# Turning rows and contexts round: 64 TensorE transposes replaced by VectorE squares of 32 and small transfers, in a four-layer cross-attention kernel

## The chip, the core and the metric

The kernel runs on one core of a Trainium2 chip. The metric is device time in microseconds (us); smaller is better. The engines are TensorE (PE in the profile, with PEld for its weight loads), VectorE (DVE), ScalarE (ACT), GpSimd (POOL) and SyncE (SP, which here only issues DMA transfers). The kernel before took 1388.54 us, the median of three runs (1388.54 to 1392.53).

## The reference

Four layers, each an attention of 4 x 256 tokens (256 wide) over a context of 4 x 512 vectors (128 wide), then a feed-forward part. All is float32. Cut to what matters here:

```python
x = x + L0_xattn(layernorm(x), ctx, ...)   # 16 heads of 16, normalised heads, context split in two parts
x = x + L0_ffn(layernorm(x), ...)          # 64 arrows, the best 4 of each token
x = x + L1_xattn(layernorm(x), ctx, ...)   # 16 heads of 128 over 8 groups of keys and values
x = x + L1_ffn(layernorm(x), ...)          # 8 experts, 2 for each token, and a shared one
x = x + L2_xattn(layernorm(x), ctx, ...)
x = x + L2_ffn(layernorm(x), ...)          # one of two experts for each token
x = x + L3_xattn(layernorm(x), ctx, ...)
x = x + L3_ffn(layernorm(x), ...)          # 64 chosen tokens of each batch
```

A layer norm takes each token's row of 256, subtracts its mean and divides by its standard deviation. Every product with such rows on TensorE needs them turned round, with the 256 numbers along the partitions; the attention's products with the context need that turned round as well.

## The kernel before, in words

**Rows and how they are turned.** x stays in SBUF, a tile `x_sb[b]` of [128 partitions, 2, 256] for each of four batches. `Norm(b, name)` (line 908 on) takes mean and variance on VectorE and the reciprocal root on GpSimd (line 922); its `tokens()` writes the normalised rows, a tile of tag "xn" (line 927). `layernorm_T` (line 933) turns such a tile round: four TensorE transposes of 128x128 into one PSUM bank (line 939), then a copy by ScalarE into a tile of tag "xnT" (line 942). Both tags lie in the pool `lnp`, which has two buffers for each tag. `context_T` (line 901) turns a batch's context in the same way (lines 905 and 906) into `cT`.

**Order.** TensorE, ScalarE, VectorE and GpSimd run their instructions in the order in which the program writes them (a manual schedule). SyncE's transfers are placed by the scheduler. Transfers go round eight DMA semaphores, 100 to 107 in the trace, and a transfer that takes a semaphore waits for the one that used it last. A tile that takes over a buffer waits for every instruction and transfer that used the tile before it there.

**Layer 0's attention.** For each batch b there are eight slots i (four head groups, two halves of the keys each). A slot puts scores on TensorE (line 1373), calls `ahead(b, i)`, puts the products with the values of the head group before (lines 1383 and 1392), in odd slots `quotient` on VectorE (lines 1406 to 1414), and then calls `between(b, i)`, which holds steps of the next batch n = b + 1: in slot 0 the rows and the context of n are turned and `last_context` copies a part of the context on GpSimd (line 1172); in slot 1 `project_q` (line 1184) multiplies the turned rows by the query weights; in slot 2 `project_k`, in slot 3 `project_v` and sums; `scaled` (line 1271) and `transposed` follow, whose evacuations are lines 1348 to 1364. In slots 5 to 7 the norm and the rows of batch n + 1 are made. PSUM is a ring of six banks beside two for the products with the values; scores take four banks of the ring at a time.

**Attentions 1 to 3.** 32 units (batch b, pair of heads hp from 0 to 7). In a unit the queries of the next unit are made (`seven`, line 1882; `four`, lines 1891 to 1895), then the scores (line 1912), the exponentials on ScalarE (line 1915), the products with the context (line 1920). At hp 1 the next batch's norm is taken, at hp 3 its rows are made, at hp 5 they are turned, at hp 6 `x_sums` (lines 1813 to 1816) makes sums of their blocks on VectorE, and the queries of (b + 1, 0) read them during unit (b, 7). At hp 3 and 7 the output of four pairs is made as well.

**Layer 1's experts** (`beside1`): beside batch b of attention 1, batch b - 1's norm is taken at hp 3, its rows at hp 4; at hp 5 `turned1` stores the rows in DRAM (line 2179) and turns them (lines 2184 and 2185); at hp 6 `chosen` picks the experts. Beside batch 0, weights are loaded by SyncE, two transfers for each unit (`load_waiting`).

Of the kernel before, what the change touches and what calls it, by code (L numbers as in the profile page):

```python
# [9 lines left out]
F32 = mybir.dt.float32  # L10
# [7 lines left out]
P = 128  # L18
B, S, D = 4, 256, 256
# [817 lines left out]
def bounded_path(ctx: ExitStack, tc: tile.TileContext, t, out: bass.AP, over):  # L837
# [63 lines left out]
    def context_T(b):  # L901

        pt = bank("t", [P, NK, P], f"pcT{b}")
        for k in range(NK):
            nc.tensor.transpose(pt[:, k, :], c_sb[:, b, k, :], ident)
        nc.scalar.copy(cT[:, b, :], pt.rearrange("p k q -> p (k q)"))
# [38 lines left out]
    def layernorm(b, name, keep=None):  # L945
        xn = Norm(b, name).tokens(keep)
        return xn, layernorm_T(xn, name)

    def normalised(name):

        after = layernorm(0, f"{name}_0")
        for b in range(B):
            _, xnT = after
            if b + 1 < B:
                after = layernorm(b + 1, f"{name}_{b + 1}")
            yield b, xnT

    raws = {}

# [68 lines left out]
    with tc.manual_schedule(engines={E.PE, E.Activation, E.DVE, E.Pool}):  # L1028
# [552 lines left out]
        def between(b, i):  # L1581

            n = b + 1
            if n == 1:
                if i == 0:
                    for k0 in range(0, NK, 2):
                        project_k(n, k0)()
                    scale[n] = Scale(n)
                    scale[n].square(False, NC, NQK)
                    xnTs[n] = layernorm_T(xns[n], f"a0_{n}")  # L1590
                elif i == 1:
                    project_q(n)()
                    scale[n].square(False, 0, NC)
                    project_v(n)
                elif i == 2:
                    scale[n].sum()
                    scale[n].power()
                elif i == 5:
                    transposed(n, 0)
                    transposed(n, 2)  # L1600
                elif i == 6:
                    transposed(n, 4)
            elif n < B:
                if i == 0:
                    xnTs[n] = layernorm_T(xns[n], f"a0_{n}")
                    context_T(n)
                    last_context(n)
                elif i == 1:
                    project_q(n)()
                elif i == 2:  # L1610
                    for k0 in range(0, NK, 2):
                        project_k(n, k0)()
                    scale[n] = Scale(n)
                    scale[n].square(False)
                elif i == 3:
                    project_v(n)
                    scale[n].sum()
                elif i == 4:
                    scale[n].power()
                elif i == 6:  # L1620
                    transposed(n, 0)
                    transposed(n, 2)
            if n + 1 < B:
                if i == (5 if n == 1 else 6):
                    norms[n + 1] = Norm(n + 1, f"a0_{n + 1}")
                elif i == (6 if n == 1 else 7):
                    xns[n + 1] = norms[n + 1].tokens()

            i0 = 4 if b == B - 1 else 6
            if b > 0 and i in (i0, i0 + 1):  # L1630
                output0(b - 1, (i - i0,))
            if b == 1:
                if i == 0:
                    bias_rows()
                elif i == 1:
                    bias_columns()
                elif i == 2:
                    output_bias()
            if b == B - 1:
                if i == 0:  # L1640

                    mf = w0.tile([B * NK, P], F32, tag="hs", name="mf", bufs=1)
                    nc.vector.tensor_copy(mf, m8)
                    xns["mf"] = mf
                elif i == 1:
                    pmk = bank("mm", [P, B * NK], "pmk")
                    nc.tensor.transpose(pmk, xns["mf"], ident[: B * NK, : B * NK])
                    nc.vector.tensor_scalar(
                        mbias.rearrange("p b k -> p (b k)"), pmk, 1.0, -NEG, ALU.subtract, ALU.mult
                    )  # L1650
                elif i == 2:
                    score_bound()
                elif i == 3:

                    nc.vector.tensor_reduce(
                        quad[:, :32], ident.rearrange("p (a q) -> p q a", q=32), AX.X, ALU.add
                    )
                    for j in range(1, 4):
                        nc.vector.tensor_copy(quad[:, 32 * j : 32 * (j + 1)], quad[:, :32])
            if b == B - 1:  # L1660
                if i in (0, 2, 6):
                    norms["f", i // 2] = Norm(min(i // 2, 2), f"f0_{min(i // 2, 2)}")
                if i in (1, 3, 7):
                    xns["f", i // 2] = norms["f", i // 2].tokens()
                if i in (3, 5):
                    k = (i - 3) // 2
                    xnTs["f", k] = layernorm_T(xns["f", k], f"f0_{k}")
                if i == 4:
                    arrows[0] = Arrows(0)
                    arrows[0].vectors()  # L1670
                if i == 5:
                    arrows[0].routes()
# [111 lines left out]
    def attention(L, m_sb, n_sb, first_xnT=None, after=None, at_end=None, chunk=None, within=None):  # L1784
# [11 lines left out]


        with tc.tile_pool(name=f"att{L}", bufs=2) as ap:
            xnTs, xns, xxs, norms, qTs, pqs, outs, sums = {}, {}, {}, {}, {}, {}, {}, {}
            units = [(b, hp) for b in range(B) for hp in range(H // 2)]  # L1800
            m_x = ap.tile([P, H // 2, 3, P], F32, tag="m_x", name=f"m_x{L}", bufs=1)
            n_x = ap.tile([P, H // 2, 3, P], F32, tag="n_x", name=f"n_x{L}", bufs=1)
# [220 lines left out]
            for n, (b, hp) in enumerate(units):  # L2023
                if b + 1 < B:
                    if hp == 1:
                        norms[b + 1] = Norm(b + 1, f"a{L}_{b + 1}")
                    elif hp == 3:
                        xns[b + 1] = norms[b + 1].tokens()
                if n == 0:
                    first_queries(1)  # L2030
                    x_sums(0)
                elif n + 1 < len(units):
                    queries(*units[n + 1])
                if b + 1 < B and hp == 5:
                    xnTs[b + 1] = layernorm_T(xns[b + 1], f"a{L}_{b + 1}")
                if b + 1 < B and hp == 6:
                    x_sums(b + 1)
                if b == 0:
                    m_sums((hp + 2) % (H // 2))
                if n:  # L2040
                    summed(*units[n - 1], *half)

                last, i = ((b, 0), hp - 4) if hp >= 4 else ((b - 1, 1), hp)
                prev = last[0] >= 0
                h0 = 4 * last[1]
                if prev and i >= 2:
                    for k in (2 * i - 4, 2 * i - 3):
                        o_sums(last[0], h0 + k, nc.gpsimd)
                half = heads(b, hp)
                if prev and i == 0:  # L2050
                    quotients(*last)
                if prev and i in (1, 2):
                    for k in (2 * i - 2, 2 * i - 1):
                        divided(last[0], h0 + k, nc.gpsimd)
                if b == 0 and hp < 6:
                    n_sums(hp)
                if (b, hp) == (1, 0):
                    n_sums(6)
                    n_sums(7)
                if prev and i == 3:  # L2060
                    out = Output(*last)
                    if last != (B - 1, 0):
                        out.products()
                        out.add()
                if after:
                    after(b, hp)
# [108 lines left out]
    nc.vector.memset(taken[:, 0, :], 0.0)  # L2175
    xnT1 = {}

    def turned1(b, xn):
        nc.sync.dma_start(xd[b * S : (b + 1) * S, :].rearrange("(c p) d -> p c d", p=P), xn)
        xnT1[b] = fx.tile([P, ND, S], F32, tag=f"xnT{b}", name=f"xnT_f1_{b}")  # L2180
        pt = bank("t", [P, ND, S], f"pxn_f1_{b}")
        for c in range(NC):
            for d in range(ND):
                nc.tensor.transpose(pt[:, d, c * P : (c + 1) * P], xn[:, c, d * P : (d + 1) * P], ident)
        nc.scalar.copy(xnT1[b], pt)
# [51 lines left out]
    def beside1(b, hp):  # L2237
        if b == 0:
            load_waiting(2)
        if b > 0:  # L2240
            if hp == 3:
                ahead1[b] = Norm(b - 1, f"f1_{b - 1}")
            elif hp == 4:
                ahead1[b] = ahead1[b].tokens()
            elif hp == 5:
                turned1(b - 1, ahead1[b])
            elif hp == 6:
                chosen(b - 1)

# [1192 lines left out]
```

## Time and profile before

| what | value |
| --- | --- |
| median of 3 runs | 1388.54 us |
| the profiled execution's own time | 1389.42 us |
| its span in the profile | 1387.6 us |
| TensorE busy | 1374.4 us, 7261 matmuls |
| VectorE, GpSimd, ScalarE busy | 886.8, 684.8, 580.8 us |
| granted TensorE clock, mean | 0.998 |
| DMA packets | 50849, 47.10 MB |
| transposes of rows (line 939), all of attention's tiles | 64, 273 ns each in the group's row |
| SyncE's transfers | 153 |

A timeline line gives the start, the length, the engine, the line of the kernel, the operation, the tile it writes and those it reads, and how many instructions are merged; in brackets stands the idle time before it and what ended it. Matmuls are pipelined, so the durations of neighbours overlap. A "windows" line gives a stretch, its length, the busy time of each engine, then the granted TensorE clock and the share and rate of the DMA engines.

### The profile page before, as it was taken

The page shows a single profiled execution, that of the slowest core. Times are in us where ns is not written, and L with a number is a line of the kernel's source. Part 1 is how long each engine was busy: PE and PEld are TensorE (multiplying, and loading weights), DVE is VectorE, ACT ScalarE, POOL GpSimd, SP SyncE. Part 2 cuts the span into 40 slices and gives each one's busy share as a digit, 9 for nine tenths or more (in the row PEclk, how much of TensorE's full clock was granted, in tenths as well). Part 3 has the DMA queues.
Part 4 walks back from the last instruction along what each step waited for, and adds up shares of the span by engine and source line. Part 5 has one row for each costly group of instructions (what it writes and reads, how often), then busy time and mean ns, then how long its engine had stood idle before and what let it go on. Part 6 is the DMA issues. An engine that isn't in the chain of part 4 may idle for free.

```text
span 1387.6 us, 19978 instructions
## 1 busy us (share of the span) xinstructions
PE 1374.4 (99%) x7261; PEld 906.5 (65%) x7261; DVE 886.8 (64%) x2026; ACT 580.8 (42%) x1148; POOL 684.8 (49%) x829
## 2 busy tenths in 40 slices
PE   8999999999999999999999999999999999999998
PEld 7665676566656667887565666666875656666667
DVE  6667863666666557655666756558656758566675
ACT  5776454433343333256434333333264334333331
POOL 4223433466564445232577654556315675445561
PEclk9999999999999999999999999999999999999999
DMA  5000220300000000272110000000342000000001
GB/s 169 2 1 2 76 77 16 75 26 1 9 0 9 0 9 30 51 231 74 39 54 8 16 1 8 1 0 16 112 125 65 9 4 4 0 1 0 1 0 34
DMA packets 50849, 47.10 MB, mean 34 GB/s; under 512 B 8755, under 2 KB 46868, under 8 KB 50742
## 3 DMA queue, kind: packets, MB, share of 16 engines
q1 hardware_dynamic: 46838, 37.74, 9.2%
q0 software_dynamic: 2544, 6.95, 1.8%
q8 instruction: 60, 0.98, 0.3%
q10 hardware_dynamic: 1360, 1.05, 0.2%
q14 instruction: 47, 0.39, 0.1%
HBM read 38.78 MB, written 6.95 MB: 33 GB/s over the span
## 4 chain that ended last, share of the span: by engine, by line
PE 94%; POOL 2%; DVE 2%; DMA 1%; issue 1%; ACT 0%; DVEq 0%; ACTq 0%; POOLq 0%
PE ps L1912 23%; PE po L1920 23%; PE paq L1882 6%; PE pao L1882 5%; PE pbq L1882 4%; PE pbo L1882 4%; PE ps L1373 3%; PE po L1383 2%; PE paf L1457 2%; PE pyf L1507 2%; PE pgu L2459 2%; PE psh L2281 1%; PE py L2006 1%; PE pm L987 1%; PE pn L1003 1%
## 5 line engine op out<-in xcount | busy, mean ns | idle before, releaser
L1931 POOL TENSOR_TENSOR half<-pT 128x1024 f32<-128x1024 f32 x93 | 218.4, 2348 | 288.3 <-ACT pT L1915 215.9
L1912 PE MATMUL ps<-qT,cT 128*128 128x512 f32 x768 | 345.6, 593 | 0.0
L1920 PE MATMUL po<-pT,c_sb 128*128 128x512 f32 x768 | 345.3, 592 | 0.0
L1915 ACT ACTIVATE pT<-ps,mbias 128x512 f32<-128x512 f32 x384 | 264.0, 687 | 155.1 <-PE ps L1912 141.0
L1920 PEld LDWEIGHTS po<-pT,c_sb 128*128 128x128 f32 x768 | 145.8, 190 | 183.2 <-issue 183.2
L1912 PEld LDWEIGHTS ps<-qT,cT 128*128 128x128 f32 x768 | 138.9, 190 | 138.4 <-issue 136.3
L1924 ACT COPY oT<-po 128x512 f32<-128x512 f32 x96 | 56.3, 586 | 265.2 <-PE po L1920 265.2
L1967 POOL TENSOR_TENSOR oT<-oT,wide 128x512 f32<-128x512 f32 x84 | 106.8, 1292 | 0.0
L1892 DVE TENSOR_TENSOR qT<-qT,paq 128x128 f32<-128x128 f32 x90 | 25.5, 283 | 96.0 <-ACT qT L1891 96.0
L1377 ACT ACTIVATE pT<-ps 128x512 f32<-128x512 f32 x128 | 66.0, 602 | 26.3 <-PE ps L1373 26.0
L1939 DVE TENSOR_TENSOR half<-half 128x512 f32<-128x512 f32 x96 | 71.8, 748 | 2.7 <-POOL half L1929 2.5
L1941 DVE STREAM_TRANSPOSE turned<-half 128x512 f32<-128x512 f32 x96 | 68.3, 711 | 6.3
L1892 DVE TENSOR_TENSOR w<-w,pao 128x128 f32<-128x128 f32 x21 | 6.0, 285 | 103.0 <-ACT w L1891 103.0
L1882 PE MATMUL paq<-xnT_a,m_sb 128*128 128x128 f32 x360 | 71.4, 280 | 0.0
L1882 PE MATMUL paq<-xx,m_x 128*128 128x128 f32 x360 | 69.6, 275 | 0.0
L1882 PEld LDWEIGHTS paq<-xnT_a,m_sb 128*128 128x128 f32 x360 | 57.2, 192 | 16.7 <-issue 8.7
L1945 DVE TENSOR_REDUCE sums<-turned 128x16 f32<-128x512 f32 x96 | 65.9, 686 | 3.3
L1882 PE MATMUL pao<-n_x,ox 128*128 128x128 f32 x336 | 65.0, 275 | 0.0
L1891 ACT COPY qT<-paq 128x128 f32<-128x128 f32 x90 | 24.0, 266 | 94.0 <-PE paq L1882 93.0
L1895 DVE TENSOR_TENSOR qT<-qT,pbq 128x384 f32<-128x384 f32 x90 | 49.9, 554 | 9.7 <-DVE qT L1894 0.5
L1882 PEld LDWEIGHTS paq<-xx,m_x 128*128 128x128 f32 x360 | 54.7, 192 | 0.0
L1966 DVE STREAM_TRANSPOSE wide<-rz 128x512 f32<-128x512 f32 x84 | 54.4, 685 | 0.0
(490 smaller groups left out, 2545.7 us busy)
## 6 DMA issues: line engine op xcount, KB each, us to landing
wq<-in_L_wqT SPq DMA_DIRECT2D x11, 512.0 KB
wo<-in_L_wo SPq DMA_DIRECT2D x11, 512.0 KB
yd<-yr SPq DMA_DIRECT2D x20, 128.0 KB
xd<-xn_f SPq DMA_DIRECT2D x8, 256.0 KB
w<-in_F_w SPq DMA_DIRECT2D x4, 512.0 KB
wk<-in_L_wkT SPq DMA_DIRECT2D x11, 128.0 KB
wv<-in_L_wvT SPq DMA_DIRECT2D x11, 128.0 KB
yd<-yb SPq DMA_DIRECT2D x9, 128.0 KB
```

Source lines behind the costliest of these rows:

```text
L1377: nc.scalar.activation(pT[kp][:, j], ps[j], AF.Exp)
L1882: nc.tensor.matmul(p[:, at, :], lhsT=lhsT, rhs=rhs, start=(k == 0 and at == 0), stop=(k == len(of) - 1 and i == which[-1]),)
L1912: nc.tensor.matmul(ps, lhsT=cT[:, b, k * P : (k + 1) * P], rhs=qT, start=True, stop=True)
L1915: nc.scalar.activation(pT[:, k, :], ps, AF.Exp, bias=mbias[:, b, k : k + 1])
L1920: nc.tensor.matmul(po, lhsT=c_sb[:, b, k, :], rhs=pT[:, k], start=(k == 0), stop=(k == NK - 1))
L1924: done["head"] = nc.scalar.copy(raw, po).ins
L1931: nc.gpsimd.tensor_tensor(half, pT[:, 0:2], pT[:, 2:4], ALU.add)
L1939: nc.vector.tensor_tensor(part, half[:, 0], half[:, 1], ALU.add)
L1941: nc.vector.transpose(turned.rearrange("p f i -> p (f i)"), part)
L1945: nc.vector.tensor_reduce(sums[b, hp // 4][:, hp % 4, :], turned, AX.X, ALU.add)
L1966: nc.vector.transpose(wide, rzs[b, hp // 4][:, hp % 4, :, None].to_broadcast([P, NB, 32]))
L1967: eng.tensor_tensor(outs[b, hp], outs[b, hp], wide.rearrange("p f i -> p (f i)"), ALU.mult)
```

## The change

VectorE can turn squares of 32x32 within 32 partitions. The change turns rows in that way: one VectorE instruction for each half of a row tile turns all its squares and writes them, ordered by their destination, into a new tile of tag "xn"; then 16 transfers on SyncE's queue, each from 32 partitions to 32 partitions, bring the squares to the partitions where they belong. It is done for the rows of batches 1 to 3 in attentions 1 to 3, for batches 0 to 2 of layer 1's experts, and in layer 0 for the rows and the contexts of batches 2 and 3. The first batches keep their transposes.

The steps move with it. In layer 0 the next but one batch's context is turned in slot 3, its norm taken in slot 4, and its rows made and turned in slot 5 of the batch before; slot 0 keeps `last_context` only. In the attentions the rows are turned at hp 3, where they are made, and for the experts at hp 4.

```diff
-    def normalised(name):
...
+    def turned_aside(dst, src, name):
+
+        y = lnp.tile([P, 4, 4, 32], F32, tag="xn", name=f"y_{name}")
+        nc.vector.transpose(
+            y.rearrange("p q n s -> p n q s"), src.rearrange("p (n q s) -> p n q s", q=4, s=32)
+        )
+        to = dst.rearrange("p (n i s) -> p i n s", i=4, s=32)
+        for i in range(4):
+            for q in range(4):
+                nc.sync.dma_start(to[32 * q : 32 * q + 32, i], y[32 * i : 32 * i + 32, q])
+
+    def layernorm_aside(xn, name, dst=None):
+
+        xnT = lnp.tile([P, ND, S], F32, tag="xnT", name=f"xnT_{name}") if dst is None else dst
+        y = lnp.tile([P, 4, ND, NC, 32], F32, tag="xn", name=f"y_{name}")
+        for c in range(NC):
+            nc.vector.transpose(
+                y[:, :, :, c].rearrange("p q d s -> p d q s"), xn[:, c, :].rearrange("p (d q s) -> p d q s", d=ND, s=32)
+            )
+        to = xnT.rearrange("p d (c i s) -> p i d c s", c=NC, s=32)
+        for i in range(4):
+            for q in range(4):
+                nc.sync.dma_start(to[32 * q : 32 * q + 32, i], y[32 * i : 32 * i + 32, q])
+        return xnT
...
             elif n < B:
                 if i == 0:
-                    xnTs[n] = layernorm_T(xns[n], f"a0_{n}")
-                    context_T(n)
                     last_context(n)
...
             if n + 1 < B:
-                if i == (5 if n == 1 else 6):
+                if i == 3:
+                    turned_aside(cT[:, n + 1, :], c_sb[:, n + 1].rearrange("p k c -> p (k c)"), f"c{n + 1}")
+                if i == 4:
                     norms[n + 1] = Norm(n + 1, f"a0_{n + 1}")
-                elif i == (6 if n == 1 else 7):
-                    xns[n + 1] = norms[n + 1].tokens()
+                elif i == 5:
+                    xnTs[n + 1] = layernorm_aside(norms[n + 1].tokens(), f"a0_{n + 1}")
...
                     elif hp == 3:
-                        xns[b + 1] = norms[b + 1].tokens()
+                        xnTs[b + 1] = layernorm_aside(norms[b + 1].tokens(), f"a{L}_{b + 1}")
...
-                if b + 1 < B and hp == 5:
-                    xnTs[b + 1] = layernorm_T(xns[b + 1], f"a{L}_{b + 1}")
...
-    def turned1(b, xn):
+    def turned1(b, xn, aside=False):
...
+        if aside:
+            layernorm_aside(xn, f"f1_{b}", xnT1[b])
+            return
...
             elif hp == 4:
-                ahead1[b] = ahead1[b].tokens()
-            elif hp == 5:
-                turned1(b - 1, ahead1[b])
+                turned1(b - 1, ahead1[b].tokens(), True)
```

More of the change, by code (lines that the diff above doesn't have):

```diff
@@ L947, in layernorm @@
         return xn, layernorm_T(xn, name)
-    def normalised(name):
[L951 to L956, printed above, removed]
+    def turned_aside(dst, src, name):
[19 more added lines that the diff above has]
+        return xnT
     raws = {}
@@ L1798, in attention @@
         with tc.tile_pool(name=f"att{L}", bufs=2) as ap:
-            xnTs, xns, xxs, norms, qTs, pqs, outs, sums = {}, {}, {}, {}, {}, {}, {}, {}
+            xnTs, xxs, norms, qTs, pqs, outs, sums = {}, {}, {}, {}, {}, {}, {}
             units = [(b, hp) for b in range(B) for hp in range(H // 2)]
```

## The prediction, made before the changed kernel was run

> **What bounds the kernel now.** I read the page first, then the timeline of TensorE in an attention, then all engines in layer 0's attention (22 to 118 us), SyncE's timeline, and the windows with the granted clock.
>
> ```profile
> PE 1374.4 (99%) x7261; PEld 906.5 (65%) x7261; DVE 886.8 (64%) x2026; ACT 580.8 (42%) x1148; POOL 684.8 (49%) x829
> ...
> PE 94%; POOL 2%; DVE 2%; DMA 1%; issue 1%; ACT 0%; DVEq 0%; ACTq 0%; POOLq 0%
> ```
>
> TensorE is busy for 99% of the span and carries 94% of the chain that ended last, so an instruction taken from it is worth its time on that engine, and a wait given to it is lost in full. A row's duration is not that time, because matmuls overlap. The start times give it:
>
> ```profile
> 349.06 0.60 PE L939 MATMUL pxn_a<-ident,xn_a 128*128 128x128 f32 x4
> 349.50 3.60 PE L1912 MATMUL ps<-qT,cT 128*128 128x512 f32 x8
> ```
>
> Four transposes have a mean duration of 273 ns in their group, but the next group starts 0.44 us after them: 0.11 us each.
>
> **What is removed.** 64 TensorE transposes: 36 for rows in attentions 1 to 3 (three batches, four each), 12 for batches 0 to 2 of layer 1's experts (0.43 us a group, 356.37 to 356.80), 16 in layer 0 (rows and context, batches 2 and 3). Attentions: 9 x 0.44 = 4.0 us. Experts: 3 x 0.43 = 1.3 us. Layer 0 is read where it stands, first batch 2, then batch 3:
>
> ```profile
> 39.35 0.69 DVE L1414 TENSOR_TENSOR o<-po,z 128x512 f32<-128x512 f32 x1
> ...
> 49.30 0.65 PE L939 MATMUL pxn_a<-ident,xn_a 128*128 128x128 f32 x4
> ...
> 49.80 0.60 PE L905 MATMUL pcT<-ident,c_sb 128*128 128x128 f32 x4
> ...
> 50.33 1.37 PE L1373 MATMUL ps<-qT,kT 32*128 32x256 f32 x16
> ...
> 53.05 1.99 PE L1184 MATMUL pq<-wq,xnT_a 128*128 128x256 f32 x8
> ```
>
> ```profile
> 81.26 0.42 PE L939 MATMUL pxn_a<-ident,xn_a 128*128 128x128 f32 x2
> ...
> 82.24 0.66 PE L905 MATMUL pcT<-ident,c_sb 128*128 128x128 f32 x4
> ...
> 82.83 1.15 PE L1373 MATMUL ps<-qT,kT 32*128 32x256 f32 x16
> ...
> 85.33 1.99 PE L1184 MATMUL pq<-wq,xnT_a 128*128 128x256 f32 x8
> ```
>
> From 49.30 to the next scores is 1.03 us; from 81.26 it is 1.57 us, 0.22 of it a wait. So 2.6 us in layer 0 and 7.9 us in all. Here a rule of the Trainium skill is weighed: "TensorE: Matmul & The Clock Gate", Part 4: PE-mode transpose, gives about 275 ns for one in a kernel, and "VectorE: DVE Perf Modes", Rules for kernel authors, sends a 128x128 transpose to TensorE where PSUM may take it. At 275 ns the 64 would be worth 17.6 us; by the start times here they are worth 7. I take the start times; the second rule then matters, because what replaces them isn't cheap. The 16 copies by ScalarE (0.59 us each, 9.4 us) go too, at no gain: ScalarE is busy 42% and isn't on the path. The function normalised isn't called on this path.
>
> **What is added, on VectorE.** 28 turns of 128x256 and 2 of 128x512. The row of 128x512 turns says 0.71 us. None shows 128x256: between 0.36 (half) and 0.71; I take 0.40, as adds go from 0.69 to 0.41 with the same halving. Sum 12.6 us. VectorE is 64% busy; in an attention it idles 3.6 us before the queries' sums of one unit (259.4), so at hp 3 the 0.8 us lie there. With that cover gone it would be 0.8 us on each of 9 batches. Layer 0 is below.
>
> **What is added, on SyncE.** 16 groups of 16 transfers of 16 KB, in runs of 128 bytes, one queue. The trace has no transfer from SBUF to SBUF. Nearest are eight small ones in a row:
>
> ```profile
> 12.71 4.45 SPq L1075 DMA_DIRECT2D wo<-in_L_wo  x8
> ```
>
> Run without a gap they take 0.42 us, 0.47 from start to start; behind one of 128 rows the next takes 0.43, so 0.476. Bounds: 0.36 (the shortest, 0.31 plus the 0.04 between) and 0.63 (after a big one). Small transfers land 1.5 to 1.7 us after their start by the landing records. A group: 15 x 0.476 + 1.6 = 8.8 us; bounds 6.8 and 11.6. The packets themselves are small: 192-byte ones take 15 ns, so 8 per engine and transfer is nothing beside the issue.
>
> Attentions: rows are turned at the start of hp 3 and first read by the sums for the queries at hp 6, two to three units of at least 8.4 us and an output of 6.2 us later. Behind those sums on VectorE the softmax sums are queued. 8.8 us is covered more than twice. Experts: from the end of hp 4 to the end of hp 6 are 17 us, for store, turn and group some 11. The experts' store of rows moves from hp 5 to hp 4 and stands ahead of its group on SyncE (0.4 us, counted). The second tile of turned rows in attention 1 (hp 4) must wait for the first one's transfers (hp 3), 20 us earlier: no wait. Weight loads of attention 1 shift by up to 7.6 us on SyncE; the last is issued at 293 us and the experts begin at 583. All zero.
>
> New waits of TensorE for eight DMA semaphores: line 1327, which reads a tile of eight transfers, shows five wait instructions, 0.11 us apart, under matmuls still queued, and no idle TensorE before it. I take zero; uncovered, 0.5 us each at some 16 places, 8 us.
>
> **Layer 0, where it goes wrong.** The new tiles share the tag "xn", which has two buffers. In slot i=3 the context is turned into one; at i=5 the rows take the other, and their turned copy needs the first again, until all 16 context transfers have landed. So two groups stand one behind the other. Batch 2: VectorE ends the quotient of i=3 at 40.04, turns the context to 40.8; group to 49.6; turn of rows to 50.4 (VectorE, ready at 46.2 after the norm moved here, 1.4, a quotient, 2.5, a qT half, 0.8, and the rows, 0.7, stands 3.4 us); group to 59.2; project_q at 59.3 instead of 53.05: +6.2 us, the 1.03 included. Behind the standing turn are queued the kT evacuations (lines 1359, 1360); their PSUM bank is one of six in rotation, so the scores of the next slot stop to about 51.8, and project_q then stands until 59.3. GpSimd's last_context, still at i=0 (before it starts at 51.55), finds the context landed at 49.6. Batch 3:
>
> ```profile
> 67.59 0.21 DVE L1249 TENSOR_SCALAR hv<-hv 128x96 f32<-128x96 f32 x1
> ...
> 74.34 0.81 DVE L1348 TENSOR_SCALAR qT<-pT,cols 128x512 f32<-128x512 f32 x1
> ...
> 74.38 1.78 PE L1373 MATMUL ps<-qT,kT 32*128 32x256 f32 x16
> ```
>
> The context is turned from 67.8 to 68.5, its group ends at 77.3, the rows are turned by 78.1, line 1348 starts then instead of at 74.34. The scores at 74.38 need its bank, as their 1.78 us in place of 1.15 shows, so they end 3.8 us later; less 1.57 is +2.2 us (by the transfers alone project_q at 87.0 against 85.33 is +1.7). Layer 0: +8.4 us.
>
> **The clock.** One stretch of this trace has a half clock:
>
> ```profile
> core 0: us, PE busy (x) PEld busy (x) DVE busy (x) ACT busy (x) POOL busy (x), PEclk, DMA share, GB/s
> ...
> 15.90:19.30 3.40, 1.32 (x8) 0.68 (x6) 3.21 (x10) 2.82 (x9) 1.11 (x5) 1.00 0.32 68
> 19.30:22.70 3.40, 3.19 (x20) 2.67 (x24) 2.56 (x6) 1.41 (x4) 0.00 (x0) 0.50 0.86 277
> ```
>
> After a window of 3.4 us with TensorE busy for 1.32, the next ran at 0.50. The skill's "TensorE: Matmul & The Clock Gate", What's actually happening, wants an idle window of about 3.4 us for that; by the page, stalls of 3 us cost nothing more, by the row a window busy for under four tenths costs half of the next, 1.7 us. The row decides. Batch 2's stall of nearly 3 us before project_q makes one such window: +1.7; batch 3's may or may not: 0.
>
> **Sum.** +8.4 + 1.7 - 5.3 = +4.8 us. The profiled run took 1389.42 (span 1387.6 and 1.8 around it), giving 1394.2; the median of the runs is 0.9 lower, giving 1393.4; I say 1393.5. With both bounds: interval 0.36 gives layer 0 +2.9, no half clock, 1386.1; interval 0.63 gives +19.2 and two half-clock windows +3.4, 1405.9.
>
> **Rivals.**
> 1. Everything lands in time: the other side. It decides in layer 0: the group's time must fall to 5.1 us (40.8 + 2 x 5.1 + 0.9 is 52.0, where project_q would stand), an interval of 0.23. Then 7.9 us are saved: 1380.6. For it speaks that SBUF has no DRAM to wait for; against, that no burst in the trace is issued below 0.36.
> 2. Break-even: at an interval of 0.40 a group takes 7.6 us, layer 0 loses 3.9 us at batch 2 and 1.0 at batch 3, and the rest gives 5.3: 1388.1. For it speaks that the first transfers of bursts take 0.31 to 0.38; against, that later ones take 0.42 and more.
> 3. Heavier: intervals of 0.6 and the half clock after both stalls: groups of 10.6 us, so 15.2 + 3.4 - 5.3 = +13.3, 1401.8. Uncovered waits of TensorE would end there too.
>
> **Chances.** My case 0.52, three quarters of it over the bound; break-even 0.22; all in time 0.13; heavier 0.13. A measurement of this kernel tells about 0.3% (4.2 us) from no change. So faster 0.16, within 0.3% 0.29, slower 0.55. The range goes from 1384 (break-even's good side) to 1402.
>
> **What would show it.** Right: in attentions a scores group follows the queries at once at hp 5; SyncE intervals near 0.48 and landings near 1.6; a turn by VectorE at about 46 us of layer 0 waiting for a DMA; project_q (line 1184 of before) waiting for its rows' DMA for some 3 us; a half-clock window near 60 us. Wrong: rows landed before project_q, a second buffer not needed, or TensorE idle before the queries of attentions 1 to 3.

## The result and the profile after

The changed kernel takes 1406.82 us (median of 5 runs, 1406.66 to 1408.48) against 1389.14 for the kernel before in the same session: a ratio of 1.0129, 95% interval 1.0118 to 1.014. It is slower, for the reason that the prediction gives and by nearly four times as much as it gives: +17.7 us instead of +4.8, outside the range.

The profiled execution took 1408.48 us, its span is 1406.8. In layer 0 and in the attentions the line numbers are 16 higher than before: project_q is line 1200, the scores of layer 0 line 1389, those of the attentions line 1928. First busy time and the chain, as on the page of before:

```profile
PE 1373.9 (98%) x7197; PEld 903.2 (64%) x7197; DVE 899.8 (64%) x2056; ACT 571.8 (41%) x1132; POOL 685.2 (49%) x829
...
PE 91%; SPq 3%; DVE 2%; POOL 2%; DMA 1%; issue 1%; ACT 1%; DVEq 0%; ACTq 0%; POOLq 0%
```

TensorE's busy time fell by 0.5 us only: the 64 transposes went, but more of the other work ran at half clock (13.9 us of busy time in the windows at 0.50, against 3.2 before). That accounts for some 5 us; the rest of the difference was not traced. Its part of the chain fell from 94% to 91%, and SyncE, which wasn't on the chain, has 3%. Next the timeline of all engines in layer 0's attention (start, duration, engine, line, operation; in brackets the idle time ahead of it and what ended it):

```profile
39.56 0.70 DVE L952 STREAM_TRANSPOSE y_c<-c_sb 128x512 f32<-128x512 f32 x1
...
40.29 11.31 SPq L958 DMA_DIRECT2D cT<-y_c  x16
...
53.09 0.77 DVE L965 STREAM_TRANSPOSE y_a<-xn_a 128x256 f32<-128x256 f32 x2 [7.37 <-DMA cT<-y_c]
...
54.01 10.33 SPq L971 DMA_DIRECT2D xnT_a<-y_a  x16
...
65.86 3.57 PE L1200 MATMUL pq<-wq,xnT_a 128*128 128x256 f32 x8 [4.36 <-DMA xnT_a<-y_a]
...
82.10 0.70 DVE L952 STREAM_TRANSPOSE y_c<-c_sb 128x512 f32<-128x512 f32 x1
...
82.83 10.65 SPq L958 DMA_DIRECT2D cT<-y_c  x16
...
94.97 0.77 DVE L965 STREAM_TRANSPOSE y_a<-xn_a 128x256 f32<-128x256 f32 x2 [4.93 <-DMA cT<-y_c]
...
95.89 10.90 SPq L971 DMA_DIRECT2D xnT_a<-y_a  x16
...
108.31 1.97 PE L1200 MATMUL pq<-wq,xnT_a 128*128 128x256 f32 x8 [2.25 <-DMA xnT_a<-y_a]
```

This is the chain that was foretold, with every link longer. VectorE turns the contexts at 39.56. SyncE issues their 16 transfers for 11.31 us. VectorE stands for 7.37 us until they have landed, because the rows' squares need the same buffer. 10.33 us of issue follow, and project_q of batch 2 starts at 65.86, not at 53.05. Batch 3 repeats it from 82.10 on; project_q, 85.33 before, starts at 108.31. Landing is 1.8 us (median), so the four groups take 12.8, 12.0, 12.2 and 12.6 us from the end of the turn to the next step, not 8.8.

Between the traces, counted from the first matmul (at 1.52 us in both), project_q of batch 2 is 12.8 us late, that of batch 3 23.0, and the start of attention 1 22.9. From there the changed kernel gains: it is 21.7 late at the start of attention 2, 20.5 at that of attention 3, 19.2 at the last scores. The starts of attention 1, before and after:

```profile
225.86 2.31 PE L1912 MATMUL ps<-qT,cT 128*128 128x512 f32 x5
...
248.80 2.74 PE L1928 MATMUL ps<-qT,cT 128*128 128x512 f32 x6
```

In the attentions this looks as it should; these two lines answer to the pair at 349.06 of before:

```profile
371.34 0.39 PE L1898 MATMUL pbq<-xx,m_sb 128*128 128x128 f32 x2
371.56 3.60 PE L1928 MATMUL ps<-qT,cT 128*128 128x512 f32 x8
```

The scores follow the last sums for the queries after 0.22 us, where four transposes and 0.44 us stood. Nothing waits for the rows' transfers. The windows (length, busy time of PE, PEld, DVE, ACT and POOL, granted clock, DMA share, GB/s):

```profile
62.30:65.71 3.41, 0.00 (x0) 0.00 (x0) 1.66 (x3) 0.00 (x0) 1.37 (x2) 1.00 0.16 24
65.71:69.13 3.42, 3.27 (x8) 2.52 (x8) 0.00 (x0) 0.00 (x0) 0.08 (x1) 0.50 0.02 5
...
591.37:594.78 3.41, 3.38 (x28) 3.13 (x28) 2.82 (x15) 0.00 (x0) 0.00 (x0) 1.00 0.00 0
594.78:598.19 3.41, 3.41 (x10) 2.69 (x9) 1.86 (x10) 0.00 (x0) 2.08 (x2) 0.50 0.13 36
```

A window with TensorE idle is followed by one at half clock, in which project_q takes 3.57 us instead of 1.99. The DMA engines are busy for 0.16 while the small transfers run, so they are far from full; experiment 6 tests whether they are what is slow. The last two lines come back below.

### The profile page after: what moved, and what is told of

It is laid out like the page before. It is cut to its first block, busy times and chain, and to the rows that moved or that the text cites. A ratio compares the mean times of both kernels' runs of the same rounds, so it can differ in the third digit from the quotient of the medians.

```text
span 1406.8 us, 20230 instructions
## 1 busy us (share of the span) xinstructions
PE 1373.9 (98%) x7197; PEld 903.2 (64%) x7197; DVE 899.8 (64%) x2056; ACT 571.8 (41%) x1132; POOL 685.2 (49%) x829
## 3 DMA queue, kind: packets, MB, share of 16 engines
q10 hardware_dynamic: 1360, 1.05, 0.2%
## 4 chain that ended last, share of the span: by engine, by line
PE 91%; SPq 3%; DVE 2%; POOL 2%; DMA 1%; issue 1%; ACT 1%; DVEq 0%; ACTq 0%; POOLq 0%
PE ps L1928 23%; PE po L1936 23%; PE paq L1898 6%; PE pao L1898 5%; PE pbq L1898 4%; PE pbo L1898 4%; PE pyf L1523 2%; PE paf L1473 2%; PE pgu L2474 2%; PE ps L1389 2%; PE psh L2296 1%; PE py L2022 1%; PE pm L1003 1%; PE pn L1019 1%; SPq L958 1%; SPq L971 1%
```

## The experiments

Theory A: the loss is issue time on SyncE, 0.64 to 0.71 us for each of the 64 small transfers of layer 0, which starts too late to be hidden. Rivals: the buffer shared by contexts and rows, TensorE's clock, the transfers in attentions and experts, the DMA engines. All kernels are edits of the changed one, except the probe.

**1. Layer 0 as before.** Attentions and experts keep the new way.

```diff
                 if i == 0:
+                    xnTs[n] = layernorm_T(xns[n], f"a0_{n}")
+                    context_T(n)
                     last_context(n)
...
-                if i == 3:
-                    turned_aside(cT[:, n + 1, :], c_sb[:, n + 1].rearrange("p k c -> p (k c)"), f"c{n + 1}")
-                if i == 4:
+                if i == (5 if n == 1 else 6):
                     norms[n + 1] = Norm(n + 1, f"a0_{n + 1}")
-                elif i == 5:
-                    xnTs[n + 1] = layernorm_aside(norms[n + 1].tokens(), f"a0_{n + 1}")
+                elif i == (6 if n == 1 else 7):
+                    xns[n + 1] = norms[n + 1].tokens()
```

Expected: 

> Layer 0 turns its late rows and contexts by TensorE again, in their old places; batches 1 to 3 of attentions 1 to 3 and layer 1's experts keep the squares of 32 and the small transfers. My theory: all of the loss is layer 0's (start of attention 1 stands 22.9 us later in the changed kernel, and everything behind it gains 3.8). Then this kernel takes 5.2 us less than before, about 1384, or 3.8 less, 1385.3, if the half-clock window in layer 1's experts (1.4 us) is there without layer 0's shift too. Each of the 9 groups of the attentions is worth -0.44, each of the 3 of the experts -0.43. Rival: what the small transfers cost in attentions and experts (weight loads stretched, SyncE busy) is hidden in the deltas after layer 0; then the time is 1389 or more.

Measured: 1387.06 us against 1389.33, ratio 0.9981 (0.9972 to 0.9991); its profiled execution took 1384.59. So layer 0 holds all of the loss and more. The time lies between my theory (1384, or 1385.3) and the rival (1389 or more). In the trace 5.56 us are gained between the start of attention 1 and the last scores (5.3 foretold); 1.05 more lie ahead of it, in an execution without before's half-clock window at 19.33. At the end 1.9 us are given back: from the start of the last group of matmuls to the end of the span it takes 7.9 us instead of 6.0. The median shows only 2.3 of the gain (more on this in experiment 7).

**2. Own buffers in layer 0.**

```diff
-        y = lnp.tile([P, 4, 4, 32], F32, tag="xn", name=f"y_{name}")
+        y = l0.tile([P, 4, 4, 32], F32, tag="yc", name=f"y_{name}")
...
-        y = lnp.tile([P, 4, ND, NC, 32], F32, tag="xn", name=f"y_{name}")
+        own = (l0, "ya") if name.startswith("a0_") else (lnp, "xn")
+        y = own[0].tile([P, 4, ND, NC, 32], F32, tag=own[1], name=f"y_{name}")
```

Expected: 

> The changed kernel, but the turned squares of layer 0's contexts and rows have a buffer each of their own, so the turn of the rows no longer waits until the 16 transfers of the contexts have landed. My theory: the group's length is SyncE's issue, 0.644 us for each transfer. Then VectorE's wait of 7.4 us is gone, but the rows' 16 transfers still queue behind the contexts' 16 on SyncE: 40.3 + 32 x 0.644 + 1.8 = 62.7, so project_q of batch 2 starts at about 62.8 instead of 65.9, and batch 3's gains as much once more: about 1400.6 to 1402. Rival 1: the shared buffer is the cause by itself; without it project_q starts at 52 to 54 and the time is 1384 to 1386. Rival 2: the loss is TensorE's half clock after the stall; then the time stays within 1 us of 1406.8.

Measured: 1409.37 us, ratio 1.0147 (1.0131 to 1.0162): no gain. All engines' timeline:

```profile
42.35 11.58 SPq L958 DMA_DIRECT2D cT<-y_c  x16
...
54.11 10.24 SPq L972 DMA_DIRECT2D xnT_a<-y_a  x16
...
65.86 3.75 PE L1201 MATMUL pq<-wq,xnT_a 128*128 128x256 f32 x8 [11.57 <-DMA xnT_a<-y_a]
```

The wait of VectorE is gone (the rows are turned at 47.70), and it doesn't matter: SyncE goes from the contexts straight to the rows, and TensorE gets both waits in one, 11.57 us. From the first issue to project_q it takes 23.5 us instead of 25.6, so the buffer was worth 2.1 us a batch. I had expected 3.1, having left out that a group can have one slow issue (here one of 1.76 us among the contexts'). The issue began 2.06 us later in this execution, after a half clock of 6.8 us at 19.33, and project_q ran at half clock in both batches (3.75 us each). The buffer falls as the cause, and so does my number.

**3. Own buffers and an early start.** With the edit of experiment 2; contexts and rows of batches 2 and 3 are inputs; nothing asks for the late place.

```diff
-                if i == 3:
+                if i == (0 if n == 1 else 1):
                     turned_aside(cT[:, n + 1, :], c_sb[:, n + 1].rearrange("p k c -> p (k c)"), f"c{n + 1}")
-                if i == 4:
+                if i == (1 if n == 1 else 2):
                     norms[n + 1] = Norm(n + 1, f"a0_{n + 1}")
-                elif i == 5:
+                elif i == (2 if n == 1 else 3):
                     xnTs[n + 1] = layernorm_aside(norms[n + 1].tokens(), f"a0_{n + 1}")
```

Expected: 

> As the kernel with own buffers, but contexts and rows of batches 2 and 3 are turned earlier: with batch 1's contexts at unit 0 of batch 0, its rows at unit 2, and one unit later each for batch 3 during batch 1 (both are inputs, so nothing they need is late). SyncE has nothing to issue from 23.9 to 40.3 us of the changed kernel. My theory: two groups take 2 x 10.3 + 1.8 = 22.4 us from about 27, so they have landed by 50, before project_q of batch 2 at 52, and batch 3's from about 57 to 80, before 85. Then layer 0's 2.6 us of TensorE come on top of the rest: 7.9 less than before, about 1381 (1379 to 1384 with a half-clock window or two). Rival: VectorE, whose turns and statistics (2.3 us a batch) now stand ahead of batch 1's scaling and quotients, becomes what layer 0 waits for; then layer 0 gains nothing or loses up to 4 us and the time is 1384 to 1389. Second rival: at these places the transfers are slower than 0.644 us because weights are still loading; then project_q waits again, over 1386.

Measured: 1384.87 us (1383.96 to 1385.26), ratio 0.9965 (0.9952 to 0.9979): 4.5 faster than before, 22 faster than the changed kernel.

```profile
27.06 10.88 SPq L958 DMA_DIRECT2D cT<-y_c  x16
...
38.11 11.23 SPq L972 DMA_DIRECT2D xnT_a<-y_a  x16
...
52.00 1.99 PE L1201 MATMUL pq<-wq,xnT_a 128*128 128x256 f32 x8
```

The two groups take their 22 us in a stretch in which SyncE had nothing to do, and project_q starts at 52.00 with no wait. That is where the prediction's first rival put it (52.0), now with transfers as slow as ever. From project_q of batch 1 to attention 1 it gains 2.3 us of the 2.6 in layer 0, so VectorE had the slack. The time is above my 1379 to 1384 and in the range of the first rival, but not for the rival's reason. At the last scores 5.4 of 7.9 are left: 1.85 went in layer 1's experts, where one half-clock window lies, and 0.35 in layer 2's, at the products with gathered rows.

**4. What sets the interval.** The kernel before with bursts of 16 transfers in attention 1 that compute nothing of the output; its time is not used.

```diff
+                        if kind in ("4x128", "pool"):
+                            queue.dma_start(w4[d, i], y4[s, q])
+                        elif kind == "8x64":
+                            nc.sync.dma_start(w8[d, i], y8[s, q])
+                        elif kind == "1x512":
+                            nc.sync.dma_start(z[d, 128 * i : 128 * i + 128], a[s, 128 * q : 128 * q + 128])
...
+                        elif kind == "own":
+                            nc.sync.dma_start(w4[d, i], y4[d, i])
+                        elif kind == "all128":
+                            nc.sync.dma_start(z[:, c], a[:, c])
+                        elif kind == "dram":
+                            nc.sync.dma_start(w4[d, i], src[:, :4])
```

Expected: 

> The kernel before with bursts of 16 transfers each in attention 1, whose result nobody uses: as in the change (32 partitions, 512 bytes in one run out, 4 runs of 128 bytes in), 1 run of 512 bytes, 1 run of 128, 2 of 256, 8 of 64, the change's own shape within the same 32 partitions, 128 partitions by 128 bytes with no shift, the same destination from DRAM, and the change's shape issued by GpSimd. Theory 1: SyncE's 0.644 us grows with the number of pieces (32 x 4 runs of 128 bytes = 128): then about 0.45 with 1 run, 0.5 to 0.55 with 2, 1.0 with 8, and the same 0.64 for 128 partitions by one run. Theory 2: going from SBUF to SBUF, or to other partitions, sets it: then all but the one from DRAM or within the partitions take 0.64 whatever the runs. Theory 3: the queue's depth sets it: the first few of a burst fast, later ones at the pace of the landings, in every shape. By GpSimd I know no price; if it is near SyncE's, two queues would halve a group.

Measured, by the view of the tile that the bursts write (minimum, median and maximum of the issue's duration, then the first and last start). In this order: the change's shape (4 runs of 128 bytes), 1 run of 512, 8 runs of 64, the change's shape within its own partitions, 128 partitions by 128 bytes, the same destination from DRAM, and the change's shape issued by GpSimd.

```profile
L2029 SPq DMA_DIRECT2D probe<-c_sb x16: 599/600/1583, 221.8 to 232.6; - x16
L2035 SPq DMA_DIRECT2D probe<-c_sb x16: 565/589/593, 234.6 to 245.4; - x16
...
L2033 SPq DMA_DIRECT2D probe<-c_sb x16: 591/609/613, 277.1 to 288.0; - x16
L2039 SPq DMA_DIRECT2D probe<-c_sb x16: 585/599/1329, 290.0 to 301.5; - x16
L2042 SPq DMA_DIRECT2D probe<-c_sb x16: 543/600/608, 303.3 to 312.9; - x16
L2045 SPq DMA_DIRECT2D probe<-in_L_wo x16: 341/430/434, 314.8 to 321.8; - x16
L2029 POOL DMA_DIRECT2D probe<-c_sb x16: 548/551/829, 521.5 to 530.0; - x16
```

Theory 2 holds in its first form, from SBUF to SBUF: there the issue takes 0.59 to 0.61 us whatever the runs, the partitions or the shift; from DRAM into the same places it takes 0.43, the number that the prediction had taken over. Theory 1 (pieces) falls, theory 3 (depth) too: the first of a burst are as slow as the others. Two bursts aren't shown (1 run of 128, 2 of 256; medians 0.589 and 0.595). Four of the seven within SBUF had one issue of 0.9 to 1.7 us, the one from DRAM none; what that is stays open. The source alone isn't it: before's stores from SBUF to its scratch tiles in DRAM, xd and yd, have medians of 0.34 to 0.37. Nor is a transfer with DRAM always cheaper: the four stores of the output that SyncE issues in before take 0.34 to 0.64. What the 0.17 us pay for stays open. GpSimd issues the same transfer in 0.55, 0.57 from start to start.

**5. Rows only.** Contexts turned by TensorE again: in layer 0 one group a batch.

```diff
                 if i == 0:
+                    context_T(n)
                     last_context(n)
...
-                if i == 3:
-                    turned_aside(cT[:, n + 1, :], c_sb[:, n + 1].rearrange("p k c -> p (k c)"), f"c{n + 1}")
```

Expected: 

> The changed kernel with layer 0's contexts of batches 2 and 3 turned by TensorE again, in their old place; the rows keep the squares of 32 and the small transfers. One group of 16 a batch in place of two, and no wait of VectorE for a buffer. Theory: a group is 10.6 us of issue and 1.5 of landing. Turned at about 47, the rows of batch 2 land at 59 and project_q stands 6 us later than before instead of 12.8; batch 3's are turned about 24 us after project_q of batch 2 and land 12 later, 4 us late instead of 10. Sum +10, half clock +1.6, -4 to -5.3 behind: about 1396 (1394 to 1398). Rival: only the pair of groups goes over the edge and one group is covered; then the time is 1384 to 1387.

Measured: 1399.94 us (1396.12 to 1401.59), ratio 1.0062 (1.0045 to 1.008).

```profile
57.83 3.75 PE L1200 MATMUL pq<-wq,xnT_a 128*128 128x256 f32 x8 [5.65 <-DMA xnT_a<-y_a]
...
97.80 3.49 PE L1200 MATMUL pq<-wq,xnT_a 128*128 128x256 f32 x8 [3.45 <-DMA xnT_a<-y_a]
```

The issue starts at 45.90, project_q at 57.83 after a wait of 5.65 us, and in batch 3 after one of 3.45. Counted from project_q of batch 1, attention 1 starts 14.4 us later than before: +10 were foretold for the waits, and 1.6 for the clock, which cost some 5. A half-clock stretch of 10.2 us, not 3.4, made project_q 3.75 us long, 13 scores behind it 2.05 instead of 1.10 and the values 1.94 instead of 1.07; batch 3's project_q took 3.49. So the time lies above my 1394 to 1398. The rival falls: one group alone isn't covered.

**6. Two queues.** Experiment 2 with every second transfer of layer 0 issued by GpSimd, at the late places.

```diff
-                nc.sync.dma_start(to[32 * q : 32 * q + 32, i], y[32 * i : 32 * i + 32, q])
+                (nc.gpsimd if q % 2 else nc.sync).dma_start(to[32 * q : 32 * q + 32, i], y[32 * i : 32 * i + 32, q])
...
-                nc.sync.dma_start(to[32 * q : 32 * q + 32, i], y[32 * i : 32 * i + 32, q])
+                queue = nc.gpsimd if q % 2 and name.startswith("a0_") else nc.sync
+                queue.dma_start(to[32 * q : 32 * q + 32, i], y[32 * i : 32 * i + 32, q])
```

Expected: 

> As the kernel with own buffers in layer 0, at the change's late places, but every second small transfer of layer 0 is issued by GpSimd (0.57 us each in the probe) and the others by SyncE. Theory: the pace of one issuing engine sets the group, so half the issues on each halves it: the contexts' take 8 x 0.65 = 5.2 us, the rows' (turned at about 47, GpSimd's rstd having waited for its own issues) 5.2 + 1.8, landed at about 54, against 65.9 in the changed kernel and 53.05 for project_q before. Layer 0 then loses 1 us at each of the two batches, and one half-clock window (1.6); with 4 to 5.3 gained behind it the time is 1386 to 1390. Rival: the transfers themselves, or the rings they share, set the pace, whoever issues them; then each queue's interval goes to about 1.2 us, project_q stays at 65 and the time at 1405 to 1409.

Measured: 1390.46 us, ratio 1.0003 (0.9994 to 1.0012): just above my 1386 to 1390, the same as before, and 19 below experiment 2, from which it differs by the queue alone. Timeline of all engines:

```profile
42.97 6.35 SPq L958 DMA_DIRECT2D cT<-y_c  x8
...
43.26 4.64 POOL L958 DMA_DIRECT2D cT<-y_c  x8
...
47.91 0.72 POOL L922 TENSOR_TENSOR rstd_a<-ve_a,neghalf 128x2 f32<-128x2 f32 x1
...
48.67 1.62 DVE L927 TENSOR_SCALAR xn_a<-x_sb,mv_a,rstd_a 128x256 f32<-128x256 f32 x2 [1.38 <-POOL rstd_a L922]
...
51.12 5.09 SPq L973 DMA_DIRECT2D xnT_a<-y_a  x8
51.56 4.37 POOL L973 DMA_DIRECT2D xnT_a<-y_a  x8 [1.42 <-issue]
...
58.09 1.97 PE L1202 MATMUL pq<-wq,xnT_a 128*128 128x256 f32 x8 [1.28 <-ACT pT L1395]
```

Both queues keep their pace side by side, so neither the transfers nor the DMA engines are the limit: the issuing engine is, or the queue that belongs to it, which no run separates (in the probe the first issues of a burst are as slow as the later ones, which speaks against a queue that fills). GpSimd's issues are instructions in its order like any others: the reciprocal root at 47.91 stands behind eight of them, and VectorE waits 1.38 us for it. Counted from project_q of batch 1, attention 1 starts 3.0 us later than before (2 foretold, and 1.6 for a half-clock window that didn't come), and what is gained behind it pays for that. This is the clearest of the runs for theory A.

**7. Attentions only.** Experiment 1 with the experts' rows turned by TensorE too, in their old two slots.

```diff
             elif hp == 4:
-                turned1(b - 1, ahead1[b].tokens(), True)
+                ahead1[b] = ahead1[b].tokens()
+            elif hp == 5:
+                turned1(b - 1, ahead1[b])
```

Expected: 

> Only attentions 1 to 3 keep the squares of 32 and the small transfers (9 groups); layer 0 and layer 1's experts turn by TensorE as before. Theory: 9 x 0.44 = 4.0 us less in the trace at the last scores group, in steps of 0.44 at each batch; in the times 2 to 4 less, since the half-clock windows fall by the phase of a grid of 3.413 us that differs from execution to execution: 1385.4 to 1387.4. Rival: what the kernel without layer 0's part lost against its trace (its median is 2.3 below before, its trace 5.6 in the same steps) comes from the small transfers; then this one stands within 1 us of before, 1388.3 to 1390.

Measured: 1388.2 us (22 runs, 1384.64 to 1392.79) against 1389.71 (35 runs, 1387.94 to 1393.08), ratio 0.9986 (0.9977 to 0.9994). Neither theory's number: 1.5 us are gained. The trace shows nine steps of 0.44 us, one behind each batch, and two losses of 0.42, in layer 1's and layer 2's experts, at the products with gathered rows: 3.1 us are left at the last scores. Much of the rest goes with the clock. Over the runs of all kernels here except the probe, 0.001 of the mean granted clock goes with 0.84 us (0.11 either way, by a fit with a level for each kernel). At equal clock this kernel stands 2.5 us below before, experiment 1 3.5 and experiment 3 6.5; but its runs had a mean clock of 0.9968, those of before 0.9979. That the clock was lower is measured; that the removed work is the reason was not tried. By the same fit the changed kernel stands 13.2 us above before at equal clock, so of its 17.7 us the clock accounts for some 4.

**8. Early, experts by TensorE.** Experiment 3 with the edit of experiment 7.

```diff
             elif hp == 4:
-                turned1(b - 1, ahead1[b].tokens(), True)
+                ahead1[b] = ahead1[b].tokens()
+            elif hp == 5:
+                turned1(b - 1, ahead1[b])
```

Expected: 

> The early kernel with layer 1's experts turned by TensorE again. Theory: their three groups are worth 3 x 0.43 = 1.3 us and nothing else hangs on them; the half-clock window in the experts' stage of some traces (1.4 us) comes by the phase of the grid and not by this part. Then the time is 1.3 above the early kernel's 1384.9: 1386.2, and 6.6 less than before in the steps of the trace. Rival: the experts' transfers bring that window; then it is 0.1 or more below the early kernel: 1384.8 or less.

Measured: 1385.28 us (1385.07 to 1388.78), ratio 0.9967 (0.9955 to 0.9979). It is 0.4 above the early kernel, with intervals that overlap, and level with it when each is set against before in its own session: by the times the experts' 1.3 us can't be told from nothing. The traces, both with a half-clock window in layer 1's experts, tell more: from the start of attention 1 to that of attention 2 it is 429.9 us here and 428.8 in experiment 3, so the experts' part is worth 1.1. The half-clock window is in this trace as well (572.44 to 575.85 us, 0.50), without the experts' transfers, so the rival falls:

```profile
572.44:575.85 3.41, 3.41 (x10) 2.70 (x9) 1.73 (x9) 0.00 (x0) 2.16 (x2) 0.50 0.16 42
```

**9. Early start, shared buffers.** Experiment 3 without the edit of experiment 2.

```diff
-                if i == 3:
+                if i == (0 if n == 1 else 1):
                     turned_aside(cT[:, n + 1, :], c_sb[:, n + 1].rearrange("p k c -> p (k c)"), f"c{n + 1}")
...
         y = lnp.tile([P, 4, ND, NC, 32], F32, tag="xn", name=f"y_{name}")
```

Expected: 

> As the early kernel, but the turned squares keep the change's shared two buffers (tag xn). The contexts of batch 2 are issued from 27.0 us and have landed at about 39.5; in the early kernel VectorE turns the rows at 33.6. Theory: the second buffer costs nothing where SyncE is what is waited for (as the late kernel with own buffers showed), but here it stops VectorE for 5.9 us ahead of batch 1's scaling (the multiplication of 1.76 us at 35.8 in the early kernel), and TensorE waits for batch 1's queries and keys: +4 to +6 at that place, perhaps a half-clock window with it (1.6). Batch 3's contexts land at 68.1, its rows are turned at 67.7, so nothing there. Together 1389 to 1392. Rival: the early start alone is what mattered, and VectorE has the slack: then 1384 to 1386, as the early kernel.

Measured: 1387.79 us (1385.9 to 1391.18), ratio 0.9995 (0.9986 to 1.0004).

```profile
39.16 0.77 DVE L965 STREAM_TRANSPOSE y_a<-xn_a 128x256 f32<-128x256 f32 x2 [6.17 <-DMA cT<-y_c]
...
42.59 1.07 PE L1357 MATMUL pT<-ident,pad 128*128 128x128 f32 x8 [2.42 <-DVE pad L1287]
...
76.08 1.06 PE L1357 MATMUL pT<-ident,pad 128*128 128x128 f32 x8 [1.23 <-DVE pad L1287]
```

VectorE stands for 6.17 us (5.9 foretold), and batch 1's scaling behind it comes late enough to cost TensorE 2.42 us here and 1.6 more until 48 us. Layer 0 ends 5.0 us later than in experiment 3: 4.0 of it stem from batch 2, inside my 4 to 6, and 0.9 from batch 3, where I had foretold nothing and the turn stands again. The times differ by 2.9 only (3.6 when each is set against before in its own session), the profiled ones by 2.0; this execution had no half-clock window before its tail, the early one's had two. The time alone, between the two theories, wouldn't decide; the trace does. The buffer, worth 2 us a batch where SyncE is waited for anyway, is worth 4 at batch 2 where it isn't.

## Why the prediction was wrong

The mechanism was right: layer 0's two groups stand one behind the other, late, in front of project_q, and the other 12 groups are hidden. (At batch 3 the transfers themselves, not the bank that the prediction named, set the end.) The step that failed is a size, "15 x 0.476 + 1.6 = 8.8 us" for a group: its 16 transfers took 12.0 to 12.8 us.

- **The interval.** "Nearest are eight small ones in a row": those were loads from DRAM, and the probe gives 0.43 us an issue for them and 0.60 for transfers within SBUF. With 0.04 between them, and one slow issue (1.50 and 1.25 us) in two of layer 0's four groups, the mean from start to start is 0.65 to 0.71 us, beyond the upper bound of 0.63 as well; landing is 1.8, not 1.6. A group takes 3.2 to 4.0 us more than predicted, above the bound of 11.6. That bound doesn't follow from its own interval: 15 x 0.63 + 1.6 is 11.1, and 15 x 0.36 + 1.6 is 7.0, not 6.8. The row that was read also holds a warning: its eight transfers, waits included, start 0.59 us apart on the average (4.45 us in all), and only the gapless ones were taken.
- **Batch 2.** Predicted project_q +6.2, measured +12.8. The two groups are 7.2 us longer than 17.6, and the contexts were turned 0.5 earlier; that makes 6.7, and 6.6 were missing.
- **Batch 3.** Predicted +2.2, by a bank that is freed late; "by the transfers alone" it was to be +1.7. With groups of 12.2 and 12.6 the transfers decide instead: contexts turned at 67.8 (plus the 14.4 of delay so far: 82.2, measured 82.10), then 0.70, 12.17, 0.77 and 12.57 give 94.0 against 85.33, +8.7. Measured: +8.6.
- **The clock.** One half-clock window at project_q, +1.7; measured +1.58. The others of layer 0 (52.06, 93.02) lie under the waits. Not foreseen: the window at 594.78 in layer 1's experts, +1.4.
- **The removed transposes.** 0.44 a batch in the attentions and 0.43 in the experts, as measured. 5.3 were to come back behind layer 0; 3.8 did, for the experts' window.
- **VectorE.** 0.40 us a turn was taken; 0.42 is measured for 128x256, 0.70 for 128x512. Nothing waits for them in attentions and experts. The eight-semaphore waits cost nothing visible.
- **The sum.** For the profiled execution 1394.2 was predicted and 1408.48 measured, 14.3 more: 6.6 at batch 2, 6.4 at batch 3, 1.4 in the experts.
- **The rivals.** "Heavier", with intervals of 0.6, was nearest and still put the time at 1401.8: its groups have 10.6 us. For "everything lands in time" I had asked for an interval of 0.23; experiment 3 reached its project_q by starting 13 us earlier. SyncE's timeline of before ends at 23.2 us for this stage, so the free place could have been seen, and with it how much hung on the interval.

## What to carry to other kernels

Price a transfer by rows with the same two ends, and where there are none let the range reach well beyond the nearest row: 64 serial issues turn 0.2 us of error into 13. Work moved to a queue is hidden only if it starts its whole serial length ahead of its reader, so look for the earliest place at which the inputs are there and the queue is empty; a second queue comes next, a buffer last. Since an issue cost the same in all seven shapes, fewer and larger transfers would be the other lever; no run here tried it. And count a stall of TensorE with what the clock takes behind it.

## What was not expected of the hardware

- An issue within SBUF costs SyncE 0.59 to 0.61 us in all seven shapes tried, from DRAM into the same places 0.43, to scratch in DRAM 0.34 to 0.37; GpSimd 0.55. Of the 124 groups of 16 in the traces without the probe, 54 had one issue of 0.86 to 1.83 us, none had two; why stays open.
- The clock changes on a grid of 3.413 us with another phase in each execution: in the changed kernel's trace the half-clock stretches begin at 52.06, 65.71, 93.02 and 594.78 us, the later ones 4, 12 and 159 steps behind the first. Over all traces, of the steps at full clock, those with TensorE busy for up to 1.57 us were followed by a half clock, one with 1.68 (in the probe) was not, of two with 1.73 and 1.72 the first was, and apart from the exception below none with 1.78 or more was (the two close ones stand below the list). So the bound lies near half a step, not at an idle step, as the Trainium skill's "TensorE: Matmul & The Clock Gate", What's actually happening, has it, and not at four tenths as the prediction read it; and so whether a stall of 2 to 3 us costs a half-clock step depends on the phase.
- One exception: the step at 591.37 counts 3.38 us busy, and the next is at 0.50. It is nearly filled by 32 products with 40 columns each (a list of the experts' rows), which run from 590.56 to 594.63. It was so in 5 of the 10 traces without the probe, with and without the experts' new transfers. That narrow products don't count as busy was not tried.

The windows of the two close cases, each with the one that follows, first from experiment 6, then from experiment 1 (columns as above):

```profile
17.62:21.04 3.42, 1.73 (x12) 1.25 (x12) 3.30 (x8) 2.71 (x8) 0.06 (x1) 1.00 0.48 76
21.04:24.45 3.41, 3.14 (x20) 2.06 (x19) 2.37 (x8) 1.57 (x5) 0.71 (x1) 0.50 0.98 379
...
15.28:18.69 3.41, 1.72 (x10) 1.03 (x8) 3.22 (x10) 2.77 (x9) 1.34 (x6) 1.00 0.29 67
18.69:22.10 3.41, 2.64 (x26) 1.87 (x27) 3.25 (x8) 1.96 (x5) 0.00 (x0) 1.00 0.81 195
```
